# A two-layer decoder on one core: an interleaved opening, shifted places in a hand-written order, and the keys and values of one entry made in the stage before

## Chip, cores and metric

The kernel runs on one core of one Trainium2 chip. The metric is the device time of one execution in microseconds (us); the time before is the median of three runs. All matrices are in 32-bit floating point.

## The reference, cut to what is computed

Eight entries (B) of 256 tokens with 256 features each, x, and a context of 256 tokens with 512 features for every entry.

```
x = x + attn16(norm(x))                      # 16 heads of 16, rotary pairs, biases
x = x + cross16(context, norm(x), bias)      # queries are the normed x, keys context[:, :256], values context[:, 256:]
x = x + expert_choice(norm(x))               # gate, clip, log, 8 Sinkhorn iterations,
                                             # each of 8 experts takes its best 32 tokens of an entry
x = x + causal16(norm(x))                    # 16 heads of 16, rotary halves, causal
x = x + cross64(norm(x), context)            # 16 heads of 64: q = x Wq; k, v = context Wkv; one null key and value;
                                             # out Wout, then a layer norm with scale and bias
x = x + moe(norm(x))                         # top-1 of 8 experts of width 704, and a shared expert of width 704:
                                             # (silu(x ws1) * (x ws3)) ws2
```

## The kernel before

The work goes through four stages: the attentions with heads of 16 together with the expert-choice layer (0 to about 470 us of the profile), the cross attention with heads of 64 (to about 941), the rest of the shared expert (to 989) and the routed experts (to the end).

**Heads of 16.** The stage is a list of 24 units: for each pair of entries two self attentions and two cross attentions (units 0 to 15), then the eight causal self attentions of layer 1 (units 16 to 23). A unit has four steps k. In a step, `Core.scores` makes scores (tile st, L334) and their exponentials on ACT (pT, L345; for the causal units followed by POOL's affine select, L350), and `Core.values` makes the products with the values (o, L371), which DVE divides and turns (attT, L397). The loop over units and steps issues the scores of the next step, then the entries of a table that are marked EARLY, then the values of this step, then the other entries of the table.

**The table.** `beside(n, k, at, ...)` puts a piece of other work into step k of unit n, and `run` issues what is there in the order of `at`. The number `at` is a place in the order and no time. All this is inside `tc.manual_schedule(engines=PINNED)`: PE, DVE, ACT, POOL and SP execute in exactly the order in which the program writes their instructions. An instruction whose operand isn't ready holds up everything behind it on its engine. The pieces are:

- for a self attention: `stats` and `norm` (layer norm of the entry, tile xn), `rows` (transposes of xn, tile tr, to xnT by ACT), `heads(t)` (projection qk, then the rotary arithmetic on DVE and POOL), `joined` (sum into qkr), `vals`, `begin` (transposes of qkr to keys and queries: tr, qps, qm), and later `out(t)` (projection ao and its sum into x);
- for a cross attention: `stats`, `norm` (xnx), `begin` (qpsx), `out` (transposes oR and DVE's sum into x);
- for each pair of entries, the 27 steps of the generator `chosen_experts`: stats and norm of both entries (xnb, on POOL), transposes, logits (lg), eight Sinkhorn iterations (PE's column sums cs, L659, then five small DVE instructions on g), the transposed gates (vps) and the search for the best 32 of each expert, three small DMAs through DRAM (slots, idx_row, by_half), cps (transposes of by_half) with the comparison `pick` on POOL, and for each entry rps (gathered rows), y (the experts' products, scaled to ys) and back (rows put back and added to x). The tables `pieces` (pairs 0 and 1), `sooner` (pair 2) and `soonest` (pair 3) give the places, counted from unit 4i + 4 for pair i.

Before the loop there is an opening: the first entry's stats, norm, rows, heads, vals, joined and so on, then its begin and first scores, and between these the second entry's.

**To the heads of 64.** In unit 20, `weights_x` opens the pools of the next stage on the right side of SBUF and loads its weights; wkv_x (4 MB) is issued by POOL. After the last unit's `out`, `tables_x` makes tables for the null key and value, with the product nvw (L839). Then `null_cross_attention` normalises entry 0 (`layernorm_T`), loads its context (ctxT), makes keys (`features`, tile fm, copied to kTx by ACT), values (`vals`, tile vps, copied to vx by ACT), the null keys (`null_key`, nps) and queries (fm again, copied to qTx by DVE), with sums of the weights on DVE between them (`sums_of_weights`, L1297, tiles tw and twq). Entries 1 to 7 are made by seven half-size products instead of eight (`seven`), each inside the attention of the entry before. In an attention, `weighted` makes scores (stx, L1419), exponentials (pTx), sums of halves on POOL (both, L1425), denominators (den) and values (ox, L1458).

The loop's last round, entry 7, closes the right-hand pools (`wproj.close()`), opens the pool "mids" in their place, and loads the shared expert's first weights into it (`load_shared`, tile ws13: two DMAs of 704 KB by SP, L990 and L991, and one copy by POOL). After the last ox come the reciprocals of the denominators (through DRAM: rd and rs), the load of ws2, the shared expert's first products (hx, L1041) and `outward` (wo).

Two helpers make a product on PE: `product` in two halves of 64 output partitions, `product4` in four quarters of 32.

Of the kernel before, what the change touches and what calls it, by code (L numbers as in the profile page):

```python
# [157 lines left out]
def plain(  # L158
# [267 lines left out]
    class SelfAttention:  # L426
# [10 lines left out]
        def norm(self):  # L437
            self.xn = work.tile([P, 2, D], F32, tag="xn", name="xn")
            for t in range(2):
                self.head = normed(  # L440
                    self.xn[:, t, :], x[:, 2 * self.b + t, :], self.mv, self.rs, t, nc.gpsimd if self.n else nc.vector
                )

        def rows(self):
# [129 lines left out]
    def turn():  # L574
        for t in range(2):
            qc, qs = rotary(bs[:, :2, :].rearrange("p i d -> p (i d)"), t, 0, work)
            nc.vector.tensor_tensor(turned[:, t, :], qc, qs, ALU.add)
# [204 lines left out]
    def weights_x():  # L782

        w_exp.close()
        wd = ctx.enter_context(tc.tile_pool(name="wd", bufs=1, side="right"))
        wproj = ExitStack()
        ctxs = wproj.enter_context(tc.tile_pool(name="ctxs", bufs=1, side="right"))
        wp = wproj.enter_context(tc.tile_pool(name="wp", bufs=1, side="right"))
        wkv_x = wp.tile([P, CTX // P, 2 * XH * XD], F32, name="wkv_x")
        wq_x = wp.tile([P, 2, XH * XD], F32, name="wq_x")  # L790
        wout_x = wd.tile([P, XH * XD // P, D], F32, name="wout_x")
        nc.gpsimd.dma_start(wkv_x, a["L1_xattn_Wkv"].rearrange("(c p) f -> p c f", p=P))
        nc.gpsimd.dma_start(wq_x, a["L1_xattn_Wq"].rearrange("(c p) f -> p c f", p=P))
        nc.gpsimd.dma_start(wout_x, a["L1_xattn_Wout"].rearrange("(c p) f -> p c f", p=P))
        nkv = a["L1_xattn_null_kv"]
        nkrow = wd.tile([P, XD], F32, name="nkrow")
        nc.sync.dma_start(nkrow, nkv[0:1, :].to_broadcast([P, XD]))
        nvcol = wd.tile([P, 1], F32, name="nvcol")
        for g in range(2):
            nc.sync.dma_start(nvcol[XD * g : XD * (g + 1), :], nkv[1:2, :].rearrange("o d -> d o"))  # L800
        lns = wd.tile([P, D], F32, name="lns")
        nc.sync.dma_start(lns, a["L1_xattn_ln_scale"].rearrange("(o d) -> o d", o=1).to_broadcast([P, D]))
        lnb = wd.tile([P, D], F32, name="lnb")
        nc.sync.dma_start(lnb, a["L1_xattn_ln_bias"].rearrange("(o d) -> o d", o=1).to_broadcast([P, D]))
        return wd, ctxs, wproj, wkv_x, wq_x, wout_x, nkrow, nvcol, lns, lnb

    def tables_x(wd, wq_x, wout_x, nkrow, nvcol):

# [36 lines left out]
            nc.gpsimd.memset(hot.rearrange("p c w -> p (c w)")[:, HP * i : nc8 * HP : 2 * HP + 1], 1.0)  # L845
        return wn, nvw, hot

    plan = {}

    def beside(n, k, at, *made):  # L850
        plan.setdefault((n, k), []).append((at, made))
# [8 lines left out]
    for n, u in enumerate(units):  # L860
        if u.__class__ is SelfAttention:
            u.n = n
            if n in (20, 22):
                beside(n - 2, 0, 80, u.stats)
                beside(n - 2, 1, EARLY, u.norm)
            else:
                beside(n - 3, 2, 80, u.stats)
                beside(n - 3, 3, EARLY, u.norm)
            beside(n - 2, 2, 30, u.rows)
            beside(n - 2, 3, 30, partial(u.heads, 0))  # L870
            beside(n - 1, 0, 30, partial(u.heads, 1))
            beside(n - 1, 1, EARLY, u.joined)
            beside(n - 1, *((2, 30) if u.layer == 0 and n % 4 else (1, 30)), partial(u.vals, 0))
            beside(n - 1, 1, 60, u.begin)
            beside(*((n, 0, 40) if u.layer else (n - 1, 2, 31) if n % 4 else (n - 1, 3, 40)), partial(u.vals, 1))
            beside(n, 3, 80, u.biased)
            for t in range(2):
                beside(n + 1, *((2 + t, 40) if u.layer else (0, 20 + t)), partial(u.out, t))
        else:
            beside(n - 1, 0, 80, u.stats, u.vals)  # L880
            beside(n - 1, 1, EARLY, u.norm)
            beside(n - 1, 1, 60, u.begin)
            beside(n + 1, *((2, 40) if n % 4 == 2 else (0, 20)), u.out)
    beside(0, 2, 40, add_up)
    beside(2, 2, 85, slot_keys)
    beside(3, 2, 50, slot_tables)

    begun = (-1, 2, 80), (0, 0, EARLY), (0, 1, 80)
    start = begun + (
        (0, 2, EARLY), (0, 3, 40), (0, 3, 41), (1, 0, 70), (1, 2, 70),  # L890
        (1, 3, 70), (2, 0, 15), (2, 1, 5), (2, 2, 10), (2, 2, 70), (2, 3, 70), (3, 0, 70), (3, 1, 45),
        (3, 2, 70), (3, 3, 85),
    )
    pieces = start + (
        (4, 1, 85), (4, 2, EARLY), (4, 3, 70), (5, 1, 10), (5, 2, 10), (5, 3, 10), (5, 3, 20), (6, 1, 10), (6, 2, 15),
    )
    sooner = start + (
        (4, 1, 84), (4, 1, 85), (4, 3, 20), (5, 0, 50), (5, 1, 35), (5, 2, 20), (5, 2, 50), (5, 3, 50), (6, 0, 50),
    )
    soonest = begun[:2] + (  # L900
        (0, 0, 80), (0, 1, EARLY), (0, 1, 65), (0, 1, 66), (0, 2, 50), (0, 2, 51),
        (0, 3, 60), (1, 0, 45), (1, 1, 10), (1, 1, 70), (1, 2, 70), (1, 3, 35), (1, 3, 70), (2, 0, 35),
        (2, 0, 70), (2, 1, 85), (2, 2, EARLY), (2, 2, 85),
        (3, 0, 10), (3, 0, 50), (3, 1, 35), (3, 2, 35), (3, 2, 50), (3, 3, 35), (4, 0, 50),
    )
    ex = [chosen_experts(2 * i, 2) for i in range(B // 2)]
    for i, made in enumerate(ex):
        for n, k, at in (pieces, pieces, sooner, soonest)[i]:
            beside(4 * i + 4 + n, k, at, partial(next, made, None))

    for u in units[:2]:
        u.n = 0
        u.stats()
        u.norm()
        if u is units[0]:
            opening = ExitStack()
            opening.enter_context(tc.issue_after(u.head.ins))
            order = ExitStack()
            order.enter_context(tc.manual_schedule(engines=PINNED))
            turn()  # L920
            u.rows()
            u.heads(0)
            u.vals(0)
            u.heads(1)
            u.joined()
            u.vals(1)
            for v in units[:2]:
                v.load()
        else:
            units[0].begin()  # L930
            units[0].core.scores(0)
            u.rows()
            u.heads(0)
            key_tables()
    for n, u in enumerate(units):
        if n == 1:
            expert_tables()
# [11 lines left out]
        for k in range(4):  # L949
            if k < 3:  # L950
                u.core.scores(k + 1)
            elif n + 1 < len(units):
                units[n + 1].core.scores(0)
            run(n, k, True)
            u.core.values(k)
            run(n, k, False)
            if (n, k) == (20, 1):
                for left in ex:
                    assert next(left, None) is None
                wd, ctxs, wproj, wkv_x, wq_x, wout_x, nkrow, nvcol, lns, lnb = weights_x()  # L960
        opening.close()
    order.close()
    for t in range(2):
        units[-1].out(t)
    wn, nvw, hot8 = tables_x(wd, wq_x, wout_x, nkrow, nvcol)
    first.close()
    banks.close()
# [282 lines left out]
    def null_cross_attention(phase):  # L1250
# [12 lines left out]
                        )  # L1263
                copy(dst[:, c2 : c2 + 2, :], ps)

        def context(b):
            t = ctxs.tile([P, CTX // P, S], F32, tag="ctxT", name="ctxT")
            nc.sync.dma_start(t, a["ctx_T"][b].rearrange("(c p) t -> p c t", p=P))
            return t

        def key_room():
            return work.tile([P, nc8, S], F32, tag="kT", name="kTx", bufs=1)

        def value_room():
            return work.tile([P, 2, XH, XD], F32, tag="vx", name="vx", bufs=1)

        def query_room():
            return work.tile([P, nc8, S], F32, tag="qT", name="qTx", bufs=1)

# [39 lines left out]
        def seven(name, s_terms, t_terms, dst, tokens_first):  # L1319
# [64 lines left out]
            product_of(4, xb, False)  # L1384
            nc.scalar.copy(of(1, 0), seen(xb))
            yield

        def vals(v, ctxT):
            for t in range(2):
                for hh in range(0, XH, 8):  # L1390
                    ps = mm.tile([P, 8, XD], F32, tag="mm", name="vps")
                    lo = (XH + hh) * XD
                    for cc in range(CTX // P):
                        product(
                            ps.rearrange("p h d -> p (h d)"),
                            ctxT[:, cc, bass.ts(t, P)],
                            wkv_x[:, cc, lo : lo + 8 * XD],
                            cc == 0,
                            cc == CTX // P - 1,
                        )  # L1400
                    nc.scalar.copy(v[:, t, hh : hh + 8, :], ps)

        def null_key(xnT):
            nps = mm.tile([P, 2, S], F32, tag="mm", name="nps")
# [139 lines left out]


        _, xnT = layernorm_T(0, work, mm, 1)
        ctxT, kT, v, qT = context(0), key_room(), value_room(), query_room()
        features(kT, wkv_x, ctxT, nc.scalar.copy)
        sums_of_weights(kv_blocks, slice(0, 3))
        sums_of_weights(q_blocks, slice(0, 3))  # L1550
        vals(v, ctxT)
        en = null_key(xnT)
        features(qT, wq_x, xnT, nc.vector.tensor_copy)
        for blocks in (kv_blocks, q_blocks):
# [1293 lines left out]
```

## Time and profile before

| | us |
|---|---|
| median of three runs | 1217.4 |
| lowest and highest run | 1216.8, 1218.6 |
| the profiled execution, its own time | 1214.46 |
| span of its trace | 1212.7 |
| PE busy | 1141.0 |
| DVE, ACT, POOL busy | 562.4, 447.6, 417.2 |
| mean granted clock of TensorE | 0.992 |

The profile is of one execution. Its span runs from the first to the last instruction; 1.8 us of the execution's time lie around it. Matmuls overlap in the array, and PE's busy time counts a stretch in which at least one is under way. A wait is given as "PE tr L291 <- DVE qkr L463": PE's transposes, issued at line 291, were held up by DVE's result qkr of line 463. Line 291 is that of a helper, so its waits are told apart by the tile that comes after the arrow. A granted clock of 0.50 means that TensorE ran at half its speed.

### The profile page before, as it was taken

To read this page: it belongs to the slowest core of one execution; us is meant where nothing else is said; L and a number is where in the kernel's file an instruction comes from. 1 tells how busy PE (TensorE), PEld (TensorE's weight loads), DVE (VectorE), ACT (ScalarE), POOL (GpSimd) and SP (SyncE) were. 2 spreads that over 40 slices of the span, in tenths; PEclk is the share of its full clock that TensorE was granted. 3 is DMA by queue.
4 is the path that set the end of the run, shared out by engine and by line. 5 is a ranking of instruction groups with operands and counts; after the bars stand their busy time and mean duration, and the time that the engine had idled before them with its cause. 6 is when DMAs were issued, how large, how long until landed. Compare 5 with 4: busy or idle time off the path is not lost.

```text
span 1212.7 us, 31559 instructions
## 1 busy us (share of the span) xinstructions
PE 1141.0 (94%) x13596; PEld 707.9 (58%) x13596; DVE 562.4 (46%) x1564; ACT 447.6 (37%) x696; POOL 417.2 (34%) x482
## 2 busy tenths in 40 slices
PE   5798989998999998999999999999999999999997
PEld 2344435444444445566666676666666486888874
DVE  4455767758775746223332433333335474222113
ACT  2666655656434361223232323232323131222220
POOL 2335344443746741132333323241416105000004
PEclk9999999999999999999999999999999999999999
DMA  7036232050200410010101010101012108599934
GB/s 223 1 127 205 91 117 91 2 171 2 83 2 11 167 71 2 18 37 18 37 19 37 18 37 19 37 19 37 19 37 72 36 2 322 217 399 404 386 123 138
DMA packets 51446, 116.76 MB, mean 96 GB/s; under 512 B 8273, under 2 KB 36417, under 8 KB 46945
## 3 DMA queue, kind: packets, MB, share of 16 engines
q1 hardware_dynamic: 45120, 98.90, 23.9%
q0 software_dynamic: 3456, 12.73, 2.9%
q10 hardware_dynamic: 2720, 3.02, 0.7%
q8 instruction: 109, 1.79, 0.6%
q14 instruction: 41, 0.33, 0.1%
HBM read 104.00 MB, written 27.93 MB: 109 GB/s over the span
## 4 chain that ended last, share of the span: by engine, by line
PE 73%; POOL 8%; DVE 7%; issue 6%; ACT 3%; DMA 2%; SPq 0%; POOLq 0%; ACTq 0%; DVEq 0%
PE h L276 7%; PE k L276 6%; PE v L276 6%; PE wo L276 5%; PE ox L1458 5%; PE stx L1419 4%; PE out L1836 4%; PE out L1653 3%; PE st L334 3%; PE h L1041 3%; PE o L371 3%; PE qk L282 3%; PE q L276 3%; PE tr L291 2%; PE fm L276 2%
## 5 line engine op out<-in xcount | busy, mean ns | idle before, releaser
L345 ACT ACTIVATE pT<-st 128x1024 f32<-128x1024 f32 (+1 forms) x128 | 110.5, 917 | 79.3 <-PE st L334 79.1
L371 PE MATMUL o<-pT,padv 128*32 128x256 f32 (+1 forms) x1536 | 100.4, 372 | 4.3 <-POOL pT L350 4.2
L1425 POOL TENSOR_TENSOR both<-pTx 128x512 f32<-128x512 f32 x64 | 82.1, 1310 | 50.5 <-issue 44.9
L371 PEld LDWEIGHTS o<-pT,padv 128*32 128x32 f32 x1536 | 40.9, 110 | 87.4 <-issue 41.7
L276 PE MATMUL h<-xrT,w 128*64 128x128 f32 (+1 forms) x1936 | 87.3, 250 | 3.1 <-issue 3.1
L276 PEld LDWEIGHTS h<-xrT,w 128*64 128x64 f32 x1936 | 84.7, 137 | 6.1 <-issue 3.9
L258 POOL TENSOR_TENSOR lnrs<-lnve,mhalf 128x2 f32<-128x2 f32 x48 | 35.1, 732 | 153.2 <-DVE lnve L256 141.8
L345 ACT ACTIVATE pT<-st,kbias 128x1024 f32<-128x1024 f32 x64 | 67.8, 1112 | 36.7 <-PE st L334 36.7
L1423 ACT ACTIVATE pTx<-stx 128x1024 f32<-128x1024 f32 x64 | 62.2, 1022 | 41.3 <-PE stx L1419 26.2
L1034 DVE TENSOR_TENSOR midr<-sl,h 128x128 f32<-128x128 f32 x102 | 29.4, 288 | 102.5 <-PE h L276 68.9
L334 PE MATMUL st<-qm,kT 32*128 32x512 f32 (+1 forms) x512 | 68.7, 606 | 5.2 <-ACT pT L345 3.3
L1033 ACT ACTIVATE sl<-h 128x128 f32<-128x128 f32 (+1 forms) x114 | 35.3, 310 | 97.8 <-PE h L276 58.8
L1419 PE MATMUL stx<-qTx,kTx 64*128 64x256 f32 x512 | 64.3, 391 | 2.5 <-ACT pTx L1423 2.5
L282 PE MATMUL qk<-l_wqkv,xnT 128*32 128x512 f32 x512 | 63.9, 616 | 2.2 <-ACT xnT L294 2.2
L1458 PE MATMUL ox<-pTx,vx 128*64 128x256 f32 x512 | 62.3, 385 | 0.0
L1513 POOL TENSOR_TENSOR oT<-oT,rs 128x512 f32<-128x512 f32 x30 | 37.3, 1274 | 66.7 <-DMA rs<-rd 66.7
L258 POOL TENSOR_TENSOR lxrs<-lxve,mhalf 128x2 f32<-128x2 f32 x8 | 5.6, 702 | 154.3 <-DVE sc L1172 123.3
L1419 PEld LDWEIGHTS stx<-qTx,kTx 64*128 64x128 f32 x512 | 46.1, 186 | 20.3 <-ACT pTx L1423 7.2
L276 PE MATMUL wo<-wout_x,oT 128*64 128x256 f32 x512 | 58.0, 379 | 0.0
L350 POOL TENSOR_SCALAR_AFFINE_SELECT pT<-pT 128x512 f32<-128x512 f32 x64 | 42.1, 671 | 39.3 <-ACT pT L345 39.3
L1458 PEld LDWEIGHTS ox<-pTx,vx 128*64 128x64 f32 x512 | 33.9, 136 | 26.4 <-issue 12.1
L1466 DVE COPY oT<-ox 128x512 f32<-128x512 f32 x16 | 11.1, 691 | 81.0 <-PE ox L1458 81.0
(361 smaller groups left out, 2195.1 us busy)
## 6 DMA issues: line engine op xcount, KB each, us to landing
w<-packs SPq DMA_DIRECT2D x22, 1408.0 KB
w<-packs SPq DMA_DIRECT2D x22, 768.0 KB
rs<-rd SPq DMA_DIRECT2D x16, 512.0 KB
packs<-L_ffn_w_eDF SPq DMA_DIRECT2D x8, 704.0 KB
packs<-L_ffn_w_eDF SPq DMA_DIRECT2D x8, 640.0 KB
packs<-L_ffn_w_eFD SPq DMA_DIRECT2D x8, 640.0 KB
ctxT<-ctx_T SPq DMA_DIRECT2D x8, 512.0 KB
wkv_x<-L_xattn_Wkv POOLq DMA_DIRECT2D x1, 4096.0 KB, 14.0
```

Source lines behind the costliest of these rows:

```text
L258: nc.gpsimd.tensor_tensor(rs[:, :n], ve[:, :n], mhalf[:, :n], ALU.pow)
L276: nc.tensor.matmul(out[h], lhsT[:, h], rhs, start=start, stop=stop, skip_group_check=True)
L282: nc.tensor.matmul(out[h : h + HP], lhsT[:, h : h + HP], rhs, start=start, stop=stop, skip_group_check=True)
L334: nc.tensor.matmul(st[:, r, :, :n], self.kT[rows, c, bass.ts(kt, P)], self.qm[rows, :, c, q0:], start=True, stop=True,)
L345: nc.scalar.activation(pT[:, :, :, :n], st[:, 2 * k : 2 * k + 2, :, :n], AF.Exp, scale=self.scale, **kb)
L350: nc.gpsimd.affine_select(out=pT[:, :, :, :P], in_=pT[:, :, :, :P], compare_op=ALU.is_ge, fill=0.0, base=0, pattern=[[0, 2], [0, 2], [1, P ...
L371: nc.tensor.matmul(o[HP * j : HP * j + HP, m, q0:], self.v_pad[:, kt, 8 * c + 2 * j + m, :], pTs[j // 2][:, j % 2, m, : S - q0], start=kt ...
L1419: nc.tensor.matmul(st[:, g, kt, :], kT[rows, c, bass.ts(kt, P)], qT[rows, c, :], start=True, stop=True)
L1423: nc.scalar.activation(pT, st, AF.Exp, scale=scale)
L1425: nc.gpsimd.tensor_tensor(both, pT[:, :, 0, :], pT[:, :, 1, :], ALU.add)
L1458: nc.tensor.matmul(o[XD * g : XD * (g + 1), i, :], v[:, kt, 2 * (c2 + i) + g, :], pT[:, g, kt, :], start=kt == 0, stop=kt == 1, skip_group ...
L1836: nc.tensor.matmul(ps[h], mid[:, i, h], sets[k % len(sets)][1][:, i, :], start=i == 0, stop=i == NFC - 1, skip_group_check=True,)
```

## The change

Three parts.

1. **Opening.** The second entry's stats, norm and rows move in between the first entry's pieces, ahead of its begin and first scores; before, they came after them. The second entry's norm was on DVE and stays there. A call that did nothing is gone.
2. **Places in the table.** For layer 1, `rows` moves from place 30 to 60 of its step. The second cross attention's `out` moves from place 20 to 40 of its step, behind `heads(1)`. The first expert norm moves from step 0 to step 1 of its unit. Two Sinkhorn iterations, cps and one back move to later places in `start`, `pieces` and `sooner`; most of `soonest` shifts.
3. **Keys and values of entry 0 of the heads of 64.** Their rooms and the context's load move out of `null_cross_attention`. A new pool kvs, on the right side and inside `wproj`, holds kTx and vx. The four pieces of keys go into the four steps of unit 23; the first piece of values goes into its last step, the second before and the others after its `out`, and all of them now lie inside the pinned order. They are made with `product4` instead of `product`. The context of entry 0 is loaded in unit 20, after the weights. `wproj` is closed in the last round as before, so the pool "mids" takes the place of kvs too.

The diff, cut to its core:

```diff
-                    self.xn[:, t, :], x[:, 2 * self.b + t, :], self.mv, self.rs, t, nc.gpsimd if self.n else nc.vector
+                    self.xn[:, t, :], x[:, 2 * self.b + t, :], self.mv, self.rs, t, nc.gpsimd if self.n > 1 else nc.vector
...
         wp = wproj.enter_context(tc.tile_pool(name="wp", bufs=1, side="right"))
+        kvs = wproj.enter_context(tc.tile_pool(name="kvs", bufs=1, side="right"))
...
+    def key_room():
+        return kvs.tile([P, nc8, S], F32, tag="kT", name="kTx")
+
+    def value_room():
+        return kvs.tile([P, 2, XH, XD], F32, tag="vx", name="vx")
+
+    def keys_x(kT, ctxT, i):
+        ps = mm.tile([P, 2, S], F32, tag="mm", name="fm")
+        for c in range(2 * i, 2 * i + 2):
+            for cc in range(CTX // P):
+                product4(ps[:, c % 2, :], wkv_x[:, cc, bass.ts(c, P)], ctxT[:, cc, :], cc == 0, cc == CTX // P - 1)
+        nc.scalar.copy(kT[:, 2 * i : 2 * i + 2, :], ps)
+
+    def vals_x(v, ctxT, i):
+        t, hh = i // 2, 8 * (i % 2)
+        ps = mm.tile([P, 8, XD], F32, tag="mm", name="vps")
...
+        nc.scalar.copy(v[:, t, hh : hh + 8, :], ps)
...
-            beside(n - 2, 2, 30, u.rows)
+            beside(n - 2, 2, 60 if u.layer else 30, u.rows)
...
-            beside(n + 1, *((2, 40) if n % 4 == 2 else (0, 20)), u.out)
+            beside(n + 1, *((2, 40) if n % 4 == 2 else (0, 40)), u.out)
+    for k in range(4):
+        beside(23, k, 60, lambda k=k: keys_x(kv0[0], ctxT0, k))
+    beside(23, 3, 70, lambda: vals_x(kv0[1], ctxT0, 0))
...
-    begun = (-1, 2, 80), (0, 0, EARLY), (0, 1, 80)
+    begun = (-1, 2, 80), (0, 1, EARLY), (0, 1, 80)
     start = begun + (
         (0, 2, EARLY), (0, 3, 40), (0, 3, 41), (1, 0, 70), (1, 2, 70),
-        (1, 3, 70), (2, 0, 15), (2, 1, 5), (2, 2, 10), (2, 2, 70), (2, 3, 70), (3, 0, 70), (3, 1, 45),
+        (1, 3, 70), (2, 0, 15), (2, 1, 5), (2, 2, 70), (2, 3, 20), (2, 3, 70), (3, 0, 70), (3, 1, 45),
         (3, 2, 70), (3, 3, 85),
     )
     pieces = start + (
-        (4, 1, 85), (4, 2, EARLY), (4, 3, 70), (5, 1, 10), (5, 2, 10), (5, 3, 10), (5, 3, 20), (6, 1, 10), (6, 2, 15),
+        (4, 1, 85), (4, 2, EARLY), (5, 0, 60), (5, 1, 10), (5, 2, 10), (5, 3, 10), (5, 3, 20), (6, 1, 10), (6, 3, 10),
     )
     sooner = start + (
-        (4, 1, 84), (4, 1, 85), (4, 3, 20), (5, 0, 50), (5, 1, 35), (5, 2, 20), (5, 2, 50), (5, 3, 50), (6, 0, 50),
+        (4, 1, 84), (4, 1, 85), (5, 0, 20), (5, 0, 50), (5, 1, 35), (5, 2, 50), (5, 3, 10), (5, 3, 60), (6, 0, 50),
     )
...
-        (0, 0, 80), (0, 1, EARLY), (0, 1, 65), (0, 1, 66), (0, 2, 50), (0, 2, 51),
-        (0, 3, 60), (1, 0, 45), (1, 1, 10), (1, 1, 70), (1, 2, 70), (1, 3, 35), (1, 3, 70), (2, 0, 35),
+        (0, 2, 35), (0, 2, 36), (0, 3, 10), (0, 3, 50),
+        (1, 0, 10), (1, 0, 70), (1, 1, 35), (1, 1, 70), (1, 2, 70), (1, 3, 35), (1, 3, 70), (2, 0, 35),
         (2, 0, 70), (2, 1, 85), (2, 2, EARLY), (2, 2, 85),
-        (3, 0, 10), (3, 0, 50), (3, 1, 35), (3, 2, 35), (3, 2, 50), (3, 3, 35), (4, 0, 50),
+        (3, 0, 70), (3, 1, 50), (3, 2, 35), (3, 3, 10), (3, 3, 35), (4, 0, 10), (4, 0, 50),
...
+    first_u.rows()
+    first_u.heads(0)
+    second_u.stats()
+    first_u.vals(0)
+    first_u.heads(1)
+    second_u.norm()
+    first_u.joined()
+    first_u.vals(1)
+    second_u.rows()
+    first_u.begin()
+    first_u.core.scores(0)
+    second_u.heads(0)
+    key_tables()
...
+                ctxT0, kv0 = context(0), (key_room(), value_room())
         opening.close()
-    order.close()
+    vals_x(kv0[1], ctxT0, 1)
     for t in range(2):
         units[-1].out(t)
+    for i in (2, 3):
+        vals_x(kv0[1], ctxT0, i)
+    order.close()
...
-        ctxT, kT, v, qT = context(0), key_room(), value_room(), query_room()
-        features(kT, wkv_x, ctxT, nc.scalar.copy)
+        (kT, v), qT = kv0, query_room()
         sums_of_weights(kv_blocks, slice(0, 3))
         sums_of_weights(q_blocks, slice(0, 3))
-        vals(v, ctxT)
```

More of the change, by code (lines that the diff above doesn't have):

```diff
@@ L804, in weights_x @@
         nc.sync.dma_start(lnb, a["L1_xattn_ln_bias"].rearrange("(o d) -> o d", o=1).to_broadcast([P, D]))
-        return wd, ctxs, wproj, wkv_x, wq_x, wout_x, nkrow, nvcol, lns, lnb
+        return wd, ctxs, kvs, wproj, wkv_x, wq_x, wout_x, nkrow, nvcol, lns, lnb
     def tables_x(wd, wq_x, wout_x, nkrow, nvcol):
@@ L846, in tables_x, with context @@
         return wn, nvw, hot
+    def context(b):
+        t = ctxs.tile([P, CTX // P, S], F32, tag="ctxT", name="ctxT")
+        nc.sync.dma_start(t, a["ctx_T"][b].rearrange("(c p) t -> p c t", p=P))
+        return t
+    def key_room():
[11 more added lines that the diff above has]
+        ps = mm.tile([P, 8, XD], F32, tag="mm", name="vps")
+        lo = (XH + hh) * XD
+        for cc in range(CTX // P):
+            product4(
+                ps.rearrange("p h d -> p (h d)"),
+                ctxT[:, cc, bass.ts(t, P)],
+                wkv_x[:, cc, lo : lo + 8 * XD],
+                cc == 0,
+                cc == CTX // P - 1,
+            )
+        nc.scalar.copy(v[:, t, hh : hh + 8, :], ps)
     plan = {}
@@ L894, in plain @@
     pieces = start + (
-        (4, 1, 85), (4, 2, EARLY), (4, 3, 70), (5, 1, 10), (5, 2, 10), (5, 3, 10), (5, 3, 20), (6, 1, 10), (6, 2, 15),
+        (4, 1, 85), (4, 2, EARLY), (5, 0, 60), (5, 1, 10), (5, 2, 10), (5, 3, 10), (5, 3, 20), (6, 1, 10), (6, 3, 10),
     )
     sooner = start + (
-        (4, 1, 84), (4, 1, 85), (4, 3, 20), (5, 0, 50), (5, 1, 35), (5, 2, 20), (5, 2, 50), (5, 3, 50), (6, 0, 50),
+        (4, 1, 84), (4, 1, 85), (5, 0, 20), (5, 0, 50), (5, 1, 35), (5, 2, 50), (5, 3, 10), (5, 3, 60), (6, 0, 50),
     )
-    soonest = begun[:2] + (
-        (0, 0, 80), (0, 1, EARLY), (0, 1, 65), (0, 1, 66), (0, 2, 50), (0, 2, 51),
-        (0, 3, 60), (1, 0, 45), (1, 1, 10), (1, 1, 70), (1, 2, 70), (1, 3, 35), (1, 3, 70), (2, 0, 35),
+    soonest = (-1, 2, 80), (0, 0, EARLY), (0, 0, 80), (0, 1, EARLY)
+    soonest += (
+        (0, 2, 35), (0, 2, 36), (0, 3, 10), (0, 3, 50),
+        (1, 0, 10), (1, 0, 70), (1, 1, 35), (1, 1, 70), (1, 2, 70), (1, 3, 35), (1, 3, 70), (2, 0, 35),
         (2, 0, 70), (2, 1, 85), (2, 2, EARLY), (2, 2, 85),
-        (3, 0, 10), (3, 0, 50), (3, 1, 35), (3, 2, 35), (3, 2, 50), (3, 3, 35), (4, 0, 50),
+        (3, 0, 70), (3, 1, 50), (3, 2, 35), (3, 3, 10), (3, 3, 35), (4, 0, 10), (4, 0, 50),
     )
@@ L909, in plain @@
             beside(4 * i + 4 + n, k, at, partial(next, made, None))
[L911 to L934, printed above, removed]
+    first_u, second_u = units[:2]
+    first_u.stats()
+    first_u.norm()
+    opening = ExitStack()
+    opening.enter_context(tc.issue_after(first_u.head.ins))
+    order = ExitStack()
+    order.enter_context(tc.manual_schedule(engines=PINNED))
+    turn()
+    first_u.rows()
[11 more added lines that the diff above has]
+    key_tables()
     for n, u in enumerate(units):
@@ L959, in plain @@
                     assert next(left, None) is None
-                wd, ctxs, wproj, wkv_x, wq_x, wout_x, nkrow, nvcol, lns, lnb = weights_x()
+                wd, ctxs, kvs, wproj, wkv_x, wq_x, wout_x, nkrow, nvcol, lns, lnb = weights_x()
+                ctxT0, kv0 = context(0), (key_room(), value_room())
         opening.close()
-    order.close()
+    vals_x(kv0[1], ctxT0, 1)
     for t in range(2):
         units[-1].out(t)
+    for i in (2, 3):
+        vals_x(kv0[1], ctxT0, i)
+    order.close()
     wn, nvw, hot8 = tables_x(wd, wq_x, wout_x, nkrow, nvcol)
@@ L1264, in features @@
                 copy(dst[:, c2 : c2 + 2, :], ps)
[L1266 to L1275, printed above, removed]
         def query_room():
@@ L1386, in seven @@
             yield
[L1388 to L1401, printed above, removed]
         def null_key(xnT):
```

## The prediction

> **What bounds the kernel now.** I read the page first: busy time by engine and the chain that ended last.
>
> ```profile
> PE 1141.0 (94%) x13596; PEld 707.9 (58%) x13596; DVE 562.4 (46%) x1564; ACT 447.6 (37%) x696; POOL 417.2 (34%) x482
> ...
> PE 73%; POOL 8%; DVE 7%; issue 6%; ACT 3%; DMA 2%; SPq 0%; POOLq 0%; ACTq 0%; DVEq 0%
> ```
>
> The reader is to see that TensorE is the bound and idle for only 1212.7 − 1141.0 = 71.7 us. The change removes no matmul, so it can win only idle time and time at a lower clock. Next I read the table of stretches (us from the start; time, PE busy, ..., granted clock, DMA share, GB/s):
>
> ```profile
> 0.00:24.00 24.00, 12.40 (x85) 4.65 (x86) 12.50 (x34) 4.64 (x9) 6.94 (x13) 0.95 0.88 272
> ...
> 447.00:508.00 61.00, 54.06 (x487) 30.19 (x485) 29.60 (x63) 12.08 (x19) 7.76 (x10) 0.97 0.03 10
> 508.00:920.00 412.00, 409.44 (x4565) 279.26 (x4566) 135.49 (x331) 124.50 (x179) 132.25 (x133) 1.00 0.11 27
> 920.00:989.00 69.00, 67.57 (x409) 41.02 (x404) 40.99 (x78) 24.39 (x38) 25.69 (x39) 1.00 0.17 48
> ```
>
> Most of the idle time lies ahead of 508, in the stages that the change edits; from 508 to 989 PE idles 4.0 us. Then PE's waits in the first 475 us, by the line that waits and what it waited for (total, times, longest):
>
> ```profile
> PE st L334 <- ACT pT L345: 8.5, 8, 1.5
> PE tr L291 <- DVE xn L262: 7.9, 1, 7.9
> PE tr L291 <- DVE qkr L463: 7.8, 7, 1.7
> PE cps L698 <- DMA by_half<-slots: 6.8, 3, 2.9
> PE qpsx L547 <- DVE xnx L262: 4.3, 4, 1.1
> PE o L371 <- POOL pT L350: 4.2, 5, 1.6
> PE back L282 <- DVE ys L756: 3.0, 2, 1.5
> PE tr L291 <- POOL xnb L262: 2.3, 2, 1.5
> ```
>
> No wait repeats much: these are steps placed slightly too early in a fixed order. Last, the stretches around gaps that also cost clock, and the load for the shared experts:
>
> ```profile
> 168.20:171.60 3.40, 1.24 (x13) 0.89 (x9) 1.84 (x4) 2.25 (x4) 0.00 (x0) 1.00 0.25 69
> 171.60:175.00 3.40, 3.40 (x22) 1.25 (x26) 0.17 (x1) 1.02 (x2) 2.25 (x3) 0.50 1.04 342
> ...
> 246.70:250.10 3.40, 3.40 (x28) 0.99 (x24) 0.00 (x0) 1.93 (x2) 3.21 (x4) 0.50 0.96 309
> 465.20:468.60 3.40, 3.40 (x9) 2.69 (x9) 0.26 (x4) 0.00 (x0) 0.27 (x1) 0.50 0.02 2
> ```
>
> ```profile
> 920.00:922.00 2.00, 2.00 (x23) 1.38 (x20) 1.37 (x3) 0.97 (x2) 1.94 (x4) 1.00 0.34 42
> 922.00:924.00 2.00, 1.68 (x16) 1.19 (x14) 1.69 (x5) 1.75 (x2) 1.93 (x12) 1.00 0.97 373
> 924.00:926.00 2.00, 2.00 (x20) 1.24 (x18) 0.89 (x4) 1.62 (x3) 1.51 (x4) 1.00 1.02 394
> ```
>
> A stretch with PE busy for 1.24 of 3.4 us is followed by one at clock 0.50. Shown as busy throughout, that one does about half the work: it costs some 1.7 us beside the gap. There are five such periods, the others at 21.4 and 304.7.
>
> [...]
>
> **Part 1, the opening.** In the timeline of the first 30 us, the second entry's norm and transposes follow the first scores (PE at 21.87), its qk then waits 1.49 us for ACT's xnT, and the next scores start at 28.25; PE runs 21.4 to 24.9 at half clock. After: those transposes stand before the first entry's begin, so their qk follows the first scores directly. The four transposes (some 0.6 us; two took 0.44) lie in the 1.67 us wait for qkr. On DVE the second norm (two instructions, 0.73) now stands ahead of qkr, in the 0.72 us in which DVE waits for POOL's qc: bound 0 to +0.7, taken as 0.1. I put the second scores at 25.2 to 26.0: 2.2 to 3.0 us earlier. I take **−2.5**.
>
> **Part 2, the shifted entries** (24 to 447 us). They remove no work; each moves one step in the written order of PE, ACT, DVE and POOL. Gaps at places that the change edits:
> - tr for qkr after units 4, 8, 12: 0.57 + 1.36 + 1.34 = 3.27. The cross unit's out (DVE's adds) and POOL's xnb stood ahead of the rotary arithmetic; out now comes after qk, xnb one step later.
> - cps for by_half: 2.16 + 2.92 + 1.68 = 6.76. The three small DMAs (slots, idx_row, by_half) keep their place on SP and cps is asked for later. Cover: the attention matmuls of most of one step; if it is too short, the same wait returns.
> - back for ys: 1.48 + 1.48 = 2.96; xnb: 1.49 + 0.77 = 2.26; rows at layer 1: 0.77 + 0.77 = 1.54; cs and y together about 1.0.
>
> Sum 17.8. A step moved later makes its successor late: pick, rps, ys and back follow cps and now stand closer to each other, and cs of iterations 4 and 5 are nearer to iteration 6. Bounds: 17.8 down to 5. I take 70%: **−12.5**. The half-clock periods at 171.6 and 246.7 follow the cps gaps of 169.4 and 243.3; two at 1.6 us, taken at 75%: **−2.4**. Not touched: o for POOL's pT (1.6 at 301.6, with the half clock at 304.7), st for pT, qpsx.
>
> **Part 3, keys and values of entry 0.** Before, 447 to 471 has gaps at 448.5 (0.68), 453.4 (1.54), 457.7 (0.98), 461.1 (2.17), 464.3 (0.67) and 470.4 (0.89), and half clock under nvw (16 in 5.4 us, against 3.7 as counted from the undisturbed ones). Then keys (fm x128) and values (vps x64) run without a gap, 13.7 us each. After, the four pieces of keys go into the four steps of the last unit and the values around its out. The matmuls are quarters of 32 columns instead of halves of 64: twice the instructions. On this trace 32 quarters of ao (8 products of 256) span 1.91 us, about 0.2 of it the last one's own drain: 0.21 a product, and fm's 64 products in 13.74 us are 0.215. So the quarters cost little: bound 0 to +1.5. ACT's eight copies (0.586 each) lie where ACT is busy 6.4 of 24 us. Loads: ctxT of entry 0 keeps its place on SP and wkv_x landed 14 us after its issue at 412, before 427. Gained: 1.54 + 0.98 + 2.17 + about 0.4 of the rest = 5.1, and 1.7 of clock. Given back: with the keys and values gone, nothing covers nvw's copy, the first norm, its transposes and ACT's xnT: a bubble of about 1.0 before null_key; and the queries' last PSUM tile waits for DVE's qTx behind the weight sums (7.4 us of DVE work that keys and values hid before): about 0.8. Bound for the two 0.5 to 4. Net 5.1 + 1.7 − 1.8 = 5.0; I take **−4.7**, with the quarters at 0.3.
>
> **A wait that the change adds, at the last block.** The new pool for keys and values lies on the right side, where the shared experts' pool is opened later. From the allocated addresses, the shared w1/w3 tile (11.8 KB a partition) reaches 1.9 KB into vx; before, it lay only over wkv_x and weight sums. So SP's two loads (704 KB each, issued at 920.3 before) wait for the last ox of entry 7, 940.5 in the profile of before. Behind them on SP are rd, the w2 load and rs. PE's first hx needs the first load, its third the second. From the bandwidths above, 1.44 MB had moved about 5.3 us after the issue[...]. Before, the third hx came 1.0 + 1.2 = 2.2 us after the last ox; after, 5.5: +3.3. The hole is longer than those that halved the clock: 1.7 at 70%, +1.2. POOL's memsets for this tile now come after entry 7's both, which frees PE's waits of 0.7 and 0.3 there: taken as −0.8. rs lands later, about 956 on the old scale, with wo at 960.6: hidden. Sum **+3.7**, bounds +2 to +7.
>
> **Sum.** −2.5 − 12.5 − 2.4 − 4.7 + 3.7 = −18.4. The profiled execution took 1214.5 us (span 1212.7 and 1.8 around it), which becomes 1196.1. It lies 2.9 below the median of the runs, 1217.4; on that scale the forecast is **1199.0**. Measurement tells about 0.2% (2.4 us) from no change.
>
> **Rivals.**
> - A: the waits change their names. PE's gaps reappear as waits on the next link (pT, qkr, ys), as the 8.5 us on ACT's pT hint. Only 30% of the gaps (−5.3) and 30% of the clock (−1.0) stay: −2.5 − 5.3 − 1.0 − 4.7 + 3.7 = −9.8, **1207.6**. Against it: between 156 and 230 ACT is busy 43 of 74 us, DVE 53.
> - B: all is won and the late load costs only its lower bound: −3.0 − 17.8 − 3.2 − 5.1 + 2 = −27.1, **1190.3**.
> - C, slower: moved steps stand ahead of operands that are not ready. The tables move about 40 instances of steps (rows, out, norm, two Sinkhorn iterations, cps and back of each pair, and most of the last pair's), and in a fixed order everything on PE behind such a step waits. If the removed waits return in full and each move is late by another 0.6 us on average, that is −18.4 + 14.9 + 24 = +20.5, **1238**. It decides from a mean of 0.09 us, where 40 of them eat the 3.5 us that the other parts leave. Against it: today's placing is as tight, and only some 25 of its several hundred steps wait, 0.3 to 2.9 us each.
> - The change doesn't do what it says: the instruction order of the changed kernel shows keys and values inside the last unit, so only their cover can fail; that lies in A.
>
> **How the numbers follow.** Forecast (1194 to 1204) 0.53, A (1204 to 1212) 0.28, B (1187 to 1194) 0.10, C 0.09. From 1190 to 1211 leaves out half of B, the edge of A and C: under 0.2. Faster by over 0.2%: 0.53 + 0.28 + 0.10 − 0.02 = 0.89; within 0.2%: 0.04; slower: 0.07.
>
> **What would show it.** Right: no wait of cps for by_half, tr for qkr under 5 us in total, clock 1.00 after cps, second scores near 25.5; keys inside the last attention and 447 to 508 shorter by 4 to 5 us; a hole of 3 to 6 us ahead of hx with w1/w3 as the releaser. Wrong: new waits under rps, y or cs of a size like those removed; keys' matmuls slower in quarters; hx starting 1 us after ox as before; a wait on ctxT or wkv_x in the last unit.

## The result, and the profile after

| | before | after |
|---|---|---|
| median (four runs each, us) | 1218.0 | 1198.4 |
| lowest and highest run | 1216.8, 1219.1 | 1193.5, 1198.8 |
| profiled execution, own time and span | 1214.46, 1212.7 | 1198.71, 1197.0 |
| ratio of the runs, 95% interval | | 0.983 (0.980 to 0.986) |

The change makes the kernel 1.7% faster, 1198.4 us; the forecast was 1199.0. To see where, I took marks that stand in both traces: the start of the first qpsx (first cross attention), of the last unit's second half of values (v), of the first scores of the heads of 64 (stx of entry 0), of those of entry 7, of the shared expert's third group hx x24, and of the last products out. Each start is read off PE's timeline.

| stretch | before, us | after, us | change | forecast |
|---|---|---|---|---|
| start to first qpsx | 52.01 | 48.75 | −3.26 | −2.5 |
| to v of the last unit | 398.65 | 384.69 | −13.96 | −14.9 |
| to stx of entry 0 | 57.34 | 51.52 | −5.82 | −4.7 |
| to stx of entry 7 | 413.01 | 413.00 | 0.0 | 0 |
| to hx x24 | 24.59 | 29.14 | +4.55 | +3.7 |
| to the last out | 250.07 | 250.18 | +0.1 | 0 |
| to the end | 17.07 | 19.71 | +2.6 | 0 |
| span | 1212.7 | 1197.0 | −15.7 | −18.4 |

Up to the last out the sum is −18.4. The tables of stretches between these marks split each change into idle and busy time of PE. Before:

```profile
52.01:450.66 398.65, 363.87 (x5202) 174.42 (x5206) 267.99 (x810) 219.32 (x293) 197.50 (x232) 0.99 0.26 87
```

```profile
450.66:508.00 57.34, 51.08 (x435) 28.34 (x425) 27.43 (x58) 9.45 (x16) 6.46 (x8) 0.97 0.04 10
```

```profile
921.01:945.60 24.59, 23.45 (x191) 13.29 (x189) 18.29 (x28) 10.42 (x13) 19.01 (x30) 1.00 0.26 89
```

After:

```profile
48.75:433.44 384.69, 359.09 (x5203) 174.96 (x5207) 270.41 (x810) 219.03 (x293) 199.72 (x232) 1.00 0.27 90
```

```profile
433.44:484.96 51.52, 49.68 (x627) 26.83 (x617) 22.84 (x47) 9.45 (x16) 6.47 (x8) 0.97 0.04 12
```

```profile
897.96:927.10 29.14, 25.40 (x191) 14.13 (x189) 12.80 (x27) 10.32 (x13) 16.32 (x30) 0.88 0.35 103
```

In the attentions PE's idle time falls from 34.8 to 25.6 us and its busy time, with the same matmuls, by 4.8. (Busy time is what overlapping matmuls cover together: in the page of before 1536 matmuls o of 372 ns each (the mean) keep PE busy for 100.4 us.) There is one half-clock period in this stretch (at 321.8) instead of three. By an estimate from their length and clock, 3.41 us at 0.50, two fewer explain at most 2 × 3.41 × 0.5 = 3.4 us of the 4.8, and what the other 1.4 are isn't shown. On the way to the heads of 64 idle time falls from 6.3 to 1.8. In the last block idle and busy time both grow, by 2.6 and 1.95, and the mean clock there is 0.88. PE's waits in the attentions before (52.01 to 450.66):

```profile
PE cps L698 <- DMA by_half<-slots: 6.8, 3, 2.9
PE st L334 <- ACT pT L345: 5.8, 6, 1.3
PE tr L291 <- DVE qkr L463: 4.6, 5, 1.4
...
PE o L371 <- POOL pT L350: 3.2, 4, 1.6
PE back L282 <- DVE ys L756: 3.0, 2, 1.5
PE tr L291 <- POOL xnb L262: 2.3, 2, 1.5
PE tr L291 <- POOL xn L262: 1.9, 4, 0.8
PE cs L282 <- DVE g L668: 1.1, 2, 0.8
```

And after (48.75 to 433.44), the longest and those that are new:

```profile
PE st L334 <- ACT pT L345: 7.2, 9, 1.3
...
PE cs L282 <- DVE g L668: 4.2, 4, 1.4
PE o L371 <- POOL pT L350: 4.2, 4, 1.8
PE qps L475 <- DVE ys L756: 1.5, 1, 1.5
PE rps L282 <- POOL pick L709: 1.3, 2, 1.1
PE tr L291 <- DVE qkr L463: 0.9, 1, 0.9
PE tr L291 <- POOL xnb L262: 0.7, 1, 0.7
```

The waits of cps for by_half (6.8), of back for ys (3.0) and of rows (tr for POOL's xn, 1.9) are gone. qkr has fallen from 4.6 to 0.9, xnb from 2.3 to 0.7. But cs for g has grown from 1.1 to 4.2, st and o for pT from 5.8 and 3.2 to 7.2 and 4.2, rps waits for pick, and a wait of 1.5 us for ys now falls on the transposes qps, which follow the experts' products y. Some 17 us went and some 8 came back.

The chain of waits in the last block, in order of time (start, length, what):

```profile
913.52 1.90 PE ox L1470 x16
915.43 0.02 SPq L1028
915.45 0.04 issue
915.49 4.35 DMA ws<-L_ffn_ws_DF
919.84 0.14 issue
919.98 6.62 PE hx L1079 x8
```

The last ox releases SP, SP issues the load of w1, its 704 KB take 4.35 us, and the first eight hx take 6.6 us (3.6 before), because TensorE runs at half clock (0.50) from 919.1 to 925.9, twice 3.41 us. The hole reaches 0.9 us into the first of them:

```profile
919.10:922.50 3.40, 2.52 (x3) 1.17 (x4) 2.25 (x6) 0.00 (x0) 0.56 (x2) 0.50 0.76 261
922.50:925.92 3.42, 3.42 (x5) 1.35 (x4) 1.58 (x3) 0.00 (x0) 0.00 (x0) 0.50 1.13 302
```

### The profile page after: what moved, and what is told of

The parts are those of the page before. It is cut to its first block, busy times and chain, and to the rows that moved or that the text cites. A ratio compares the mean times of both kernels' runs of the same rounds, so it can differ in the third digit from the quotient of the medians.

```text
span 1197.0 us, 31939 instructions
## 1 busy us (share of the span) xinstructions
PE 1135.5 (95%) x13788; PEld 706.5 (59%) x13788; DVE 566.2 (47%) x1564; ACT 447.5 (37%) x696; POOL 417.6 (35%) x482
## 4 chain that ended last, share of the span: by engine, by line
PE 76%; POOL 7%; issue 6%; DVE 6%; ACT 4%; DMA 1%; SPq 0%; POOLq 0%; ACTq 0%; DVEq 0%
PE h L276 7%; PE k L276 6%; PE v L276 6%; PE wo L276 5%; PE ox L1470 5%; PE stx L1431 5%; PE st L334 4%; PE out L1846 4%; PE o L371 3%; PE out L1663 3%; PE h L1079 3%; PE qk L282 3%; PE q L276 3%; ACT pT L345 2%; PE den L1446 2%
## 5 line engine op out<-in xcount | busy, mean ns | idle before, releaser
L1435 ACT ACTIVATE pTx<-stx 128x1024 f32<-128x1024 f32 x64 | 62.1, 1022 | 40.8 <-PE stx L1431 27.7
L1846 PE MATMUL out<-w,midr 128*64 128x256 f32 x408 | 47.1, 379 | 2.7 <-issue 2.7
L1470 PEld LDWEIGHTS ox<-pTx,vx 128*64 128x64 f32 x512 | 33.9, 136 | 26.4 <-issue 12.5
```

The lines of the kernel that those rows point to most:

```text
L1435: nc.scalar.activation(pT, st, AF.Exp, scale=scale)
L1470: nc.tensor.matmul(o[XD * g : XD * (g + 1), i, :], v[:, kt, 2 * (c2 + i) + g, :], pT[:, g, kt, :], start=kt == 0, stop=kt == 1, skip_group ...
L1846: nc.tensor.matmul(ps[h], mid[:, i, h], sets[k % len(sets)][1][:, i, :], start=i == 0, stop=i == NFC - 1, skip_group_check=True,)
```

## The experiments

Each was timed beside the kernel before on one chip; the ratios are to that kernel. Between chips the kernel before had medians of 1215.0 to 1218.7, so times of different groups are compared by ratio.

**The opening alone.**

```diff
     first_u.heads(0)
+    second_u.stats()
     first_u.vals(0)
     first_u.heads(1)
+    second_u.norm()
...
+    second_u.rows()
     first_u.begin()
```

> The kernel before with the interleaved opening alone. Theory (parts add up): the marks of the two traces put the opening at 3.1 us, so about 1214.5 against 1217.5, and the first cross attention's qpsx stands at 48.8 us instead of 52.0. Rival (the time before the first exponentials is made up later, behind ACT): under 1 us, about 1217.

Measured: 1210.5 against 1215.1, ratio 0.9963 (0.9948 to 0.9977). The first qpsx starts at 48.74, 3.3 us earlier; the rival falls. The other 1.3 us are not explained for sure: the profile has three half-clock periods behind the opening, against four before, which would fit.

**The table alone.**

> The kernel before with the shifted table entries alone. Theory: PE from the first qpsx to the last unit is 14.0 us shorter, so about 1203.5; the waits of cps for by_half and of back for ys are gone, cs waits for g about 4 us in total. Rival (the waits change their names once the opening is the old one): 5 us or less, 1212.

Measured: 1199.9, 0.9874 (0.9852 to 0.9896), some 15 us. From the first qpsx (52.31) to the last unit's v (437.10) it takes 384.79 us, against 384.69 with all three parts. The table does this by itself; the rival falls.

**Keys and values alone.**

> The kernel before with the keys and values of entry 0 moved alone. Theory: the way to the heads of 64 gets 5.8 us shorter and the last block 4.5 longer (a 3.4 us hole ahead of hx, half clock after it, less 2 us of den's waits): 1.3 in all, about 1216. Rival (the last block's loss is not of this part): 5.8, about 1211.7.

Measured: 1210.2, 0.9956 (0.9940 to 0.9972): 3.4 to 7.3 us less, nearer to the rival's number. Its trace doesn't support the rival's reason: hx starts 6.4 us after the start of the last group of ox, as in the changed kernel (2.95 before), and the last block takes 27.7 us instead of 24.6. The profiled execution was the slowest of the seven (1213.8), with six half-clock periods ahead of its end. Why the runs gain more than its marks give, 5.8 on the way to the heads of 64 less 3.1 in the last block, stays open.

**Opening and table without the keys.**

> The kernel before with the opening and the table, without the moved keys and values. Theory (parts add but for the clock's luck): at the marks, the opening 3.1 and the table 14 less than before, so the last unit starts some 17 us earlier, as in the changed kernel, and the way from there to the first scores of the heads of 64 is the old one: about 1200. Rival (opening and table win the same time twice): 1203 or more.

Measured: 1198.3, 0.9854 (0.9828 to 0.9880); the product of the two single ratios is 0.9838. The changed kernel on the same chip (below) has 0.9821, so keys and values added to these bring some 3 us, with an interval as wide as that. From v to stx of entry 0 it takes 57.35 us, as in the kernel before (57.34): the shortening of this stretch belongs to the keys and values alone. The product of all three single ratios is 0.9794; within the intervals the parts add.

**The pools apart.** mid0, mid1 and the routing tables leave the pool of w1/w3, which then lies over wp and the context only.

```diff
                 late = ctx.enter_context(tc.tile_pool(name="mids", bufs=1, side="right"))
-                load_shared(late)
+                behind = ctx.enter_context(tc.tile_pool(name="behind", bufs=1, side="right"))
+                load_shared(late, behind)
...
-                routing_tables(late)
+                routing_tables(behind)
```

> The changed kernel, with the shared experts' tiles mid0, mid1 and the routing tables in a pool of their own behind the pool with w1/w3 and w2, so that only the former lies over vx. Theory: w1/w3 are loaded during the last attention, hx starts 1 us after the last ox at full clock, 6.6 us less than the changed kernel: about 1191.8; den's waits stay away since POOL's memsets of mid0 and mid1 still come after its sums. Rival (the hole comes from what stands ahead on SP or POOL): no change, 1198.

Measured: 1189.1, 0.9784 (0.9765 to 0.9804). From the start of the last ox group to hx 2.94 us, from there to hx x24 4.10, against 6.52 and 7.12: 6.60 less, as forecast. The last block (the stretch begins 0.2 us ahead of its first stx) and the load's issue, from the table of stretches and the view of the tile ws:

```profile
897.96:920.70 22.74, 22.42 (x193) 13.05 (x189) 10.64 (x21) 10.37 (x14) 16.46 (x29) 1.00 0.25 90
```

```profile
L1028 SPq DMA_DIRECT2D ws<-L_ffn_ws_DF x1: 403/403/403, 895.9 to 895.9; - x1
```

PE idles 0.3 us in the whole block, at full clock; the load goes 20 us earlier. So the hole, its clock and its cause, the pool's place over vx, are shown. The edit moved w1/w3's whole pool away from vx; whether the 1.9 KB of the tile that the prediction named or the whole region of the pool made the load wait, it doesn't show.

**The memsets ahead again.** The same kernel, with mid0 and mid1 back in the first pool and the tables left behind.

> The kernel with the separate pools, but with mid0 and mid1 back in the pool that doesn't lie over vx, so that POOL's two memsets (1.1 us) run ahead of the sums of the last attention again. Theory (these memsets and the small tables behind them held den up by 2.0 us in the kernel before): from the last stx to the last ox some 0.7 to 1.1 us longer than the 15.5 of the changed kernel. Rival (den's waits came from the tables alone, or from ACT): 15.5 as before.

Measured: 1188.8, 0.9785 (0.9757 to 0.9812), 6.3 us less than the changed kernel on the same chip (below). From stx of entry 7 to the last ox group it takes 15.49 us, as with the memsets behind, and hx follows that group by 2.94 us: to move the tables alone is enough to avoid the hole.

On the 2 us of den's waits the run says less. Its memsets run at 893.9, ahead of the first stx (895.99), where POOL had been idle for 19.5 us. In the kernel before they ran at 920.7, directly followed by the tables: 3.5 us of work, up to 924.1, right ahead of POOL's sums. So in that idle stretch the memsets cost nothing; their cost in the old place wasn't tried, nor were the tables alone. An estimate from the traces: in the changed kernel POOL waits 1.92 us at that place for DVE's yx, so only some 1.6 of the 3.5 us could delay the sums, and neither the memsets (1.5) nor the tables (1.9) would have done it by themselves.

**cps alone.**

```diff
-        (4, 1, 85), (4, 2, EARLY), (4, 3, 70), (5, 1, 10), ...
+        (4, 1, 85), (4, 2, EARLY), (5, 0, 60), (5, 1, 10), ...
...
-        (4, 1, 84), (4, 1, 85), (4, 3, 20), (5, 0, 50), ...
+        (4, 1, 84), (4, 1, 85), (5, 0, 20), (5, 0, 50), ...
```

> The kernel before with one shift alone: cps (pick with it) goes from step 3 of the fifth unit to step 0 of the next for the first three pairs. Theory: the three waits for by_half (6.8 us) and the half clock after two of them (3.3) go, less about 1 for a later pick: about 9 us less than before, the largest single share of the table. Rival (rps, y or back wait instead): 3 us or less, with a new wait of rps for pick of 1 us or more at each pair.

Measured: 1212.2 against 1218.7, 0.9956 (0.9939 to 0.9972), about 5.4 us. In the view of PE's waits:

```profile
PE rps L282 <- POOL pick L709: 1.8, 2, 1.5
PE cps L698 <- DMA by_half<-slots: 1.7, 1, 1.7
```

The 1.7 is the last pair's, which has its own table: my "first three pairs" miscounted where the waits stood. Two waits (5.1 us) go: in the first pair the scores st, which stood behind cps and started 2.3 us after the end of the transposes, now start 0.1 us after it. And 1.8 comes back under rps, of which 0.5 was there. This is about a third of the table's 15 us, between theory and rival; the other shifts weren't tried alone.

**The last piece of values after the norm.**

```diff
-    for i in (2, 3):
-        vals_x(kv0[1], ctxT0, i)
+    vals_x(kv0[1], ctxT0, 2)
...
         (kT, v), qT = kv0, query_room()
+        vals_x(v, ctxT0, 3)
```

> The changed kernel with the last piece of values made after entry 0's norm of the next stage instead of before nvw. Theory (the bubble after nvw is two waits, and the second, nps for ACT's xnT, only lacks work): the wait of 0.8 us goes, the 1.04 of the transposes for xn stays, 0.8 us less than the changed kernel, up to 2.5 if the half clock at 475 goes too. Rival (the new stage's PSUM waits for the old one's last copy): the gap moves ahead of the values, no change.

Measured: 0.9815 (0.9793 to 0.9838), not told apart from the changed kernel's 0.983. In PE's timeline:

```profile
471.63 0.41 PE L291 MATMUL tr<-ident,xn 128*128 128x128 f32 x2 [1.04 <-DVE xn L262]
471.97 1.05 PE L282 MATMUL vps<-wkv_x,ctxT 128*32 128x512 f32 x2
472.94 0.44 PE L291 MATMUL tr<-ident,xn 128*128 128x128 f32 x2
```

The wait of nps (0.80) is gone, the 1.04 stands, and no half clock follows. From v to stx it takes 50.25 us instead of 51.52. Not all of this is the edit's: the second profile of the changed kernel (below) has no half clock here either and takes 50.94, so the wait's own share is 0.7. The mechanism is as forecast; the whole kernel's time can't show it.

**Halves again.** `product` in place of `product4` in keys_x and vals_x.

> The changed kernel with the keys and values of entry 0 made in halves of 64 columns again, half as many instructions. Theory (quarters stream at the same rate): each piece of keys takes 3.3 to 3.5 us as in quarters, no change within 0.5 us. Rival (instructions cost): [...]some 3 to 5 us less than the changed kernel.

Measured: 0.9872 (0.9840 to 0.9903), some 5 us more than the changed kernel's 0.983, though the intervals overlap. A piece of keys takes 3.29 us, as in quarters (3.25 to 3.31). But from v to nvw it takes 36.8 us against 35.75, without a wait in either. Where halves and quarters meet, the starts of two groups lie 0.1 to 0.2 us further apart (0.31 instead of 0.20 us ahead of a piece of keys), at seven places. So quarters save about 1.0 us here, which neither theory had. In the profiled execution half clock in the opening took another 2.5 us (first qpsx at 51.29); the rest of the 5 us stays open.

**One Sinkhorn iteration later.**

```diff
-        (1, 3, 70), (2, 0, 15), (2, 1, 5), (2, 2, 70), (2, 3, 20), (2, 3, 70), (3, 0, 70), (3, 1, 45),
+        (1, 3, 70), (2, 0, 15), (2, 1, 5), (2, 2, 70), (2, 3, 20), (3, 0, EARLY), (3, 0, 70), (3, 1, 45),
```

> The changed kernel with the sixth Sinkhorn iteration of each of the first three pairs one place later: after the next scores instead of directly after qk. Theory (the new waits of cs for g, 1.44, 1.18 and 1.18 us, come from two iterations with only qk between them): scores of 0.75 us go into each wait, about 2.2 us less than the changed kernel in sum, cs's waits near 1.8 in total instead of 4.2. Rival (DVE's chain is late anyway, or the next iteration then waits): no change.

Measured: 0.9818 (0.9795 to 0.9842); PE's wait:

```profile
PE cs L282 <- DVE g L668: 2.2, 5, 0.5
```

4.2 fell to 2.2, so the spacing is the cause of the new waits, with one small return at the iteration behind. In the time it can't be told from the changed kernel.

**The changed kernel again, and all repairs at once.**

> The changed kernel again, beside the next two on one chip: 0.983 of the kernel before. Its last 20 us (from the last products to the end) are 19.7 us in its first profile; if that is chance, some executions take 17 us there.

Measured: 1195.1, 0.9821 (0.9798 to 0.9844). The hole ahead of hx is 3.6 us, again with w1's load as the releaser. The tail takes 17.2 us in this profile, of the same program that took 19.7 in the first. DVE's timeline in the first profile, and in this one:

```profile
1184.13 0.42 DVE L1674 TENSOR_TENSOR x<-x,out 128x256 f32<-128x256 f32 x1 [4.00 <-PE out L1663]
```

```profile
1179.71 0.42 DVE L1674 TENSOR_TENSOR x<-x,out 128x256 f32<-128x256 f32 x1
```

In the first, DVE stood for 4.0 us ahead of this sum. The products that the view names had long been made (before and in the second profile the sum starts 2.9 us after the last products begin, there 6.9). What held it isn't shown. That it is chance is: one program has both, and among the other profiles four have the late sum too, one of them that of cps alone in the kernel before.

> All three repairs in one: separate pools, the last piece of values after the norm, the sixth iteration one place later. Theory (they sit at different places and add): 6.6 + 1.3 + 1.7 at the marks, about 9.5 us less than the changed kernel, 0.975 of the kernel before. Rival (the repairs share the same half-clock time): 7 us less, as with the pools alone.

Measured: 1188.8, 0.9778 (0.9754 to 0.9802), 6 us less than the changed kernel on the same chip, and 2.2% less than before. The rival is nearer: against the pools alone (0.9784) the two small repairs add nothing that the time shows, although their waits are gone in the trace (no cs wait of 0.6 or more, no nps wait). Its opening ran two periods at half clock (first qpsx at 51.38), which took back 2.6 us in the profiled execution.

## Why the prediction was right, step by step

**Opening: right.** The second scores start at 25.25, forecast 25.2 to 26.0, and qk follows the first scores directly. DVE's second norm isn't free: the moved transposes now wait 1.51 us for xn where tr waited 1.67 for qkr, so the wait only changed its name, and the first scores come 0.3 later than before (22.05 against 21.76; the working's 21.87 is a misreading). The gain is the wait of qk for xnT (1.49) and the half clock that ran ahead of it, from 21.4 to 24.9. That clock is not certain: of the ten profiles with this opening three had half clock at about 20 us again, and their first qpsx stands at 51.2 to 51.4, in the others at 48.7 to 49.5. The four profiles with the old opening have it at 49.9 to 53.5.

**Table: the sum right, its two terms not.** Gaps were forecast at −12.5 and gave −9.2 of idle time; clock was forecast at −2.4, and the busy time fell by 4.8, of which two half-clock periods fewer explain 3.4. The two misses cancel, which is luck. The waits that the steps named did go, 17 of 17.8 us; cps's cover held. What failed is the 30% set aside for returns, 5.3: some 8 came back. The largest is cs, which the step counted as a small gain while naming its risk: +3.1, one of the prediction's own signs of being wrong, though smaller than the waits removed. The others are ys under qps (+1.5), pT under st and o (+2.4) and pick under rps (+0.8).

**Keys and values: right, with a term missed.** −5.8 against −4.7. The 1.7 us of clock that the step counted came only in part: in the first profile a half-clock period at 475.4 took the place of the one under nvw (whose 16 matmuls took 3.72 us instead of 5.38), while the second has none there and takes 50.94 us, 6.4 less than before. The bubble after nvw is 1.04 + 0.80 us. The queries' wait for DVE's qTx, taken as 0.8, is absent in the first profile, where PE ran at clock 0.50 from 475.4 to 478.8, and 0.9 in the second, at full clock. That DVE caught up while PE was slower is an inference from these two. Quarters, charged 0.3, save about 1.0.

**The new wait: right in place and cause, mixed in size.** The hole and its clock cost 6.6 us against 4.5 forecast, because two half-clock periods followed each other in the profiled execution (one in the second: 5.5). The two loads, 5.3 us by the working, took 6.2: POOL's copy, which waits for the second, starts at 921.6, and SP issued the first at 915.4. Against it den's waits gave back 2.0 instead of 0.8. The reason given for them, POOL's memsets, is neither shown nor refuted.

**The tail** was in no step: +2.6 us by chance. The spans differ by 15.7 us and the medians by 19.6 because the profiled execution before was a fast one, 3.5 us below its median (the prediction allowed 2.9), while the one after lies 0.3 above its own.

**The sum is closer than its parts.** Up to the last out the measured −18.4 equals the forecast. That is luck: the four terms miss by 0.8, 0.9, 1.1 and 0.9 us, two each way.

Of the rivals, A (waits change their names) is true for 8 us of 17 and not for the rest; C (moved steps late) appears at cs and rps alone, at 0.3 to 1.4 us each. B takes 5.1 us for the third part where its terms allow 6.3 (5.1 + 1.7 − 0.5), a slip without consequence.

## What to carry to other kernels

In the fixed order here, steps moved later freed their own waits and tightened the chain behind them (some 17 us of waits went, 8 came back): look at what separates the moved step from its successor, here only one projection between two iterations, not at the step alone. A pool that outlives its old neighbour decides when the next pool in that place may be loaded: before moving buffers, check what is opened over them and who prefetches into it; this one line was worth 6.6 us, a third of the whole gain. Here gaps of 1.62 and 1.83 us were followed by 3.41 us at clock 0.50 in one execution and not in another of the same program, some 1.7 us more by estimate (half of 3.41), so judge a small repair by its wait in the trace and not by a median.

## What the runs showed of the hardware

The half-clock periods of one program differ between executions: ahead of its last 20 us the changed kernel had them at 321.8, 475.4 and 919.1 (3.41, 3.41 and 6.83 us long) in one profile and at 290.3, 324.5, 399.6 and 921.8 (3.41 us) in the other. In the clock records of each profile the starts lie whole multiples of 3.413 us apart: 321.76, 475.36 and 919.10 by 45 and 130; 290.34, 324.47, 399.57 and 921.80 by 10, 22 and 153; in the kernel before 21.44, 171.63, 246.72, 304.75 and 465.17 by 44, 22, 17 and 47. From one profile to the other they are shifted: 321.76 and 324.47 lie 2.71 us apart, no whole multiple. The gap of 1.62 us (o for POOL's pT) was followed by half clock in the second profile, at 290.3, with PE busy for 1.64 of the 3.41 us before; in the first the clock stayed at 1.00 from 287.2 to 294.5.

How long PE was busy in the 3.41 us before doesn't tell by itself whether half clock comes. In the kernel before it was busy for 0.53 to 1.66 us ahead of the five periods. In the first profile of the changed kernel it was busy for 1.74 us ahead of the one at 321.76. But in the same profile, with the gap of 1.83 us, it was busy for 1.58 of the 3.42 us from 396.85 to 400.27, and the next 3.41 us ran at 1.00; in the second profile, with that gap, half clock followed at 399.6. What decides it isn't shown. How long half clock lasts differed as well: after the hole ahead of hx, PE was busy for 2.52 of the first 3.40 us at half clock in the first profile, and another 3.42 us at half clock followed; in the second profile PE was busy throughout the 3.41 us, and full clock followed.
